# Graph attention scores: one head over all 1024 keys at a time

## The chip, the cores and the metric

The kernel runs on one core of a Trainium2 chip. The metric is the device time of one execution in microseconds; the figure for a kernel is the median over several executions. Engines are written as in the profile: PE is TensorE's matmuls and PEld its weight loads, DVE is VectorE, ACT is ScalarE, POOL is GpSimd, and SP is SyncE, which issues the transfers.

## What is computed

A batch of 16 graph elements, each with 1024 nodes of 64 features and a 1024 x 1024 adjacency matrix, goes through four layers, each with a layer norm and a ReLU ahead and a residual sum behind. Layer 0 thins the adjacency, takes weighted quantiles over the remaining neighbours of each node and applies a small network. Layer 1 takes a mean over neighbours. Layer 2 is attention with eight heads of 64 and the adjacency as a bias. Layer 3 multiplies by the adjacency once more. The change touches layer 2:

```python
qkv = jnp.einsum('bnc,kc->bnk', x, W_qkv)            # 3 x 8 heads x 64
attn = jnp.einsum('bhnd,bhmd->bhnm', q, k) * SCALE   # queries n, keys m
gamma = jnp.exp(x @ W_gamma.T + b_gamma)
attn = g0 * attn + g1 * adj[:, None]                 # g0, g1: per query
attn = jax.nn.softmax(attn, axis=-1)                 # over the 1024 keys
out = jnp.einsum('bhnm,bhmd->bnhd', attn, v).reshape(b, n, H * DIM)
return out @ W_proj.T + b_proj
```

## The kernel before

**Two streams of work.** The generator `picks()` produces layer 0. For each element it makes 96 comparison steps (8 groups of features, 2 halves of nodes, 6 quantile ranks). A step (`compare`, `bits`, `value`) puts three 2048-wide operations on DVE (`le`, `wa`, `wb`, lines 819 to 823), then matmuls `prep` and `val` (line 842) and copies on ACT. Beside the steps `make` builds the tables with the long runs of `px` matmuls (line 735), and `background` does the sorting (lines 577 to 579 forward, 609 to 612 backward) and the thinning for elements to come. For the last two elements nothing is left to sort or thin. The generator `layers()` runs layers 1, 2 and 3 of earlier elements. The loop at the end of the kernel takes turns: each step of `picks` adds 0.42 to what is due, and each part of a layer that is run takes its yielded cost from it (1.0 for one row block of layer 2). When `picks` is exhausted, `alone` is set, and the layers of the last element run by themselves with more buffers. Within this program order a scheduler fixes the order on each engine ahead of the run. Each engine works through its own list in order and waits on semaphores for the others. `adjoining` keeps a group of matmuls next to each other.

**Layer 2.** `h2T` holds the features of an element in columns: rows 0 to 63 are the normalized features h, rows 64 to 127 are h times the per-query factor g0. The loop over `pr` takes the heads in four pairs. For each pair the projections come first (line 1155): keys `kT` from rows 0 to 63 and queries `qT` from rows 64 to 127, both 128 x 1024, with head 0 of the pair in partitions 0 to 63 and head 1 in 64 to 127. Each of two halves of 512 nodes takes one key bank `pk` and one query bank `pq` of PSUM, and each is copied by ACT (line 1162). Then come the values `v`. The loop over `i` takes eight row blocks of 128 queries. In each, the adjacency rows `ad` are loaded and scaled by g1 on ACT. For each half `t` of the keys, two matmuls (line 1190) write the scores of both heads into the two banks of `sp`, one head on each row half of the array (64 rows each). For each head a DVE operation (line 1199) then forms minus the score minus the bias in `s` and takes the minimum over the half. The second half gets the minimum of the first as its starting value, through a pointer operand. The profile calls this operation CUSTOM_DVE_ANT_0 and the write of its minimum `nm` DVE_READ_ACCUMULATOR2_ANT. After both halves, ACT takes the exponential of each head's 1024 scores with the minimum as bias (line 406, `s<-s,nm`). `chunk_cols` transposes them on PE in groups of four (line 459, `pcols`), and ACT copies them to `eT` (line 462). PE multiplies with the values (line 1211, `ao`) and, after a copy, projects (line 1220, `pp`). `residual` adds the result to `xr` after every four row blocks.

**Buffers.** `sp` has one buffer of two PSUM banks; while `alone` is set the second half of the keys goes to two banks `pc` instead. The tags `pb` (two PSUM banks) and, when alone, `pa` serve the projections, transposes and products. `kT` and `qT` have one buffer each. When alone, odd pairs take theirs from the tag `q4`, which has two.

An fp32 matmul appears in the profile as two instructions, its two passes, so each score matmul counts twice in line 1190. A transpose counts once.

Of the kernel before, what the change touches and what calls it, by code (L numbers as in the profile page):

```python
# [8 lines left out]
F32 = mybir.dt.float32  # L9
# [12 lines left out]
P = 128  # L22
# [16 lines left out]
def tile_preln_adj_stack(  # L39
# [30 lines left out]
    nc = tc.nc  # L70
    B, N, D = x.shape
    C = N // P
    H = 8
    HD = W1.shape[1]
    NH = N // 512
# [5 lines left out]
    ps = ctx.enter_context(tc.tile_pool(name="ps", bufs=1, space=PSUM))  # L81
# [9 lines left out]
    def q4(name, shape=(P, N), dt=F32):  # L91
        return sb.tile(list(shape), dt, tag="q4", bufs=2, name=name)
# [7 lines left out]
    def pa(name, shape=(P, 512), dt=F32):  # L100
        return ps.tile(list(shape), dt, tag="pa", bufs=2, name=name)

    def pc_(name, shape=(P, 512), dt=F32):
        return ps.tile(list(shape), dt, tag="pc", bufs=2, name=name)


    alone = []

    def b4(name, shape=(P, N), dt=F32):
        return a4(name, shape, dt) if alone else sb.tile(list(shape), dt, tag="b4", bufs=2, name=name)  # L110

    def pb(name, shape=(P, 512), dt=F32):
        if alone and name != "pcols":
            return pa(name, shape, dt)
        return ps.tile(list(shape), dt, tag="pb", bufs=2, name=name)
# [68 lines left out]
    for c2 in range(2):  # L184
        cols = slice(c2 * BKW, (c2 + 1) * BKW)
# [177 lines left out]
    wqkv = const.tile([P, 2 * H * D], F32, name="wqkv")  # L363
# [5 lines left out]
    for e in range(2):  # L369
        rows = slice(e * D, (e + 1) * D)  # L370
# [19 lines left out]
    sb = ctx.enter_context(tc.tile_pool(name="sb", bufs=1))  # L390
# [11 lines left out]
    def bc(ap, shape):  # L402
        return ap.to_broadcast(list(shape))
# [4 lines left out]
    def adjoining(made):  # L408

        first = next(made)  # L410
        with tc.issue_after(first.ins), tc.high_priority():
            for _ in made:
                pass
# [27 lines left out]
    def to_cols(h, hT, rows):  # L441

        n = h.shape[2]
        for s in range(NH):
            pt = pb("pt", (n, 4, P))
            for c in range(4):
                nc.tensor.transpose(pt[:, c, :], h[:, 4 * s + c, :], identf)
            nc.scalar.copy(hT[rows, s * 512 : (s + 1) * 512], pt[rows].rearrange("d c p -> d (c p)"))
# [663 lines left out]
    def layer2(b, xr):  # L1112
        h = b4("h2", (P, C, 2, D))
        norm_relu(xr, h[:, :, 0, :], b2_)
        hT = sb.tile([P, N], F32, tag="hT2", bufs=1, name="h2T")
        to_cols(h[:, :, 0, :], hT, slice(0, D))
        pg = pb("pg", (P, C, 2))
        for j in range(C):
            nc.tensor.matmul(pg[:, j, :], hT[:D, j * P : (j + 1) * P], wg, start=True, stop=True)
        gm = small("gm", [P, C, 2])  # L1120
        nc.vector.tensor_tensor(gm, pg, bc(bgr[:, None, :], [P, C, 2]), OP.add)
        act(gm, gm, AF.Exp)
        g0 = small("g0", [P, C])
        nc.vector.tensor_scalar(g0, gm[:, :, 0], SCALE, None, op0=OP.mult)

        nc.vector.tensor_tensor(h[:, :, 1, :], h[:, :, 0, :], bc(g0[:, :, None], [P, C, D]), OP.mult)
        to_cols(h.rearrange("p c s d -> p c (s d)"), hT, slice(D, P))
        nc.vector.tensor_tensor(xr, xr, bc(bpr[:, None, :], [P, C, D]), OP.add)
        yield 0.7
        HW = H * D  # L1130
        late = []
        for pr in range(H // 2):

            def residual(i, att, sums):
                rows = xr[:, i : i + C // 2, :]
                rs = small("rs", [P, C // 2, 2], bufs=1)
                nc.vector.reciprocal(rs, sums)
                nc.vector.tensor_tensor(
                    att, att, bc(rs[:, :, :, None], [P, C // 2, 2, D]), OP.mult
                )  # L1140
                for e in range(2):
                    nc.vector.tensor_tensor(rows, rows, att[:, :, e, :], OP.add)

            if alone and pr % 2:
                kT, qT = q4("kT"), q4("qT")
                v = sb.tile([P, C, P], F32, tag="hT", bufs=1, name="v2")
            else:
                kT = sb.tile([P, N], F32, tag="kT", bufs=1, name="kT")
                qT = sb.tile([P, N], F32, tag="qT", bufs=1, name="qT")
                v = sb.tile([P, C, P], F32, tag="v2", bufs=1, name="v2")  # L1150
            for t in range(NH):
                hs = slice(t * 512, (t + 1) * 512)
                both = ((kT, slice(0, D), pb("pk")), (qT, slice(D, P), pb("pq")))
                adjoining(
                    nc.tensor.matmul(
                        pk, wqkv[rows, pr * P : (pr + 1) * P], hT[rows, hs],
                        start=True, stop=True,
                    )
                    for _, rows, pk in both
                )  # L1160
                for dst, _, pk in both:
                    nc.scalar.copy(dst[:, hs], pk)
            for t in range(NH):
                pv = pb("pv2", (P, 4, P))
                for c in range(4):
                    j = 4 * t + c
                    nc.tensor.matmul(
                        pv[:, c, :], hT[:D, j * P : (j + 1) * P],
                        wqkv[:D, HW + pr * P : HW + (pr + 1) * P], start=True, stop=True,
                    )  # L1170
                nc.scalar.copy(v[:, 4 * t : 4 * t + 4, :], pv)
            yield 0.5
            for i in range(C):
                if i % (C // 2) == 0:
                    att = sb.tile([P, C // 2, 2, D], F32, tag="att", bufs=1, name="att")
                    sums = small("sums", [P, C // 2, 2], bufs=2)
                ad = adj_rows(b, i)
                act(ad, ad, AF.Copy, scale=gm[:, i, 1:2])
                eTs = []
                ss = [b4("s") for _ in range(2)]  # L1180
                nms = [None, None]
                for t in range(NH):
                    hs = slice(t * 512, (t + 1) * 512)
                    if alone and t % 2:
                        sps = [pc_("sp") for _ in range(2)]
                    else:
                        sp = ps.tile([P, 2, 512], F32, tag="sp", bufs=1, name="sp")
                        sps = [sp[:, e, :] for e in range(2)]
                    adjoining(
                        nc.tensor.matmul(  # L1190
                            sps[e], qT[e * D : (e + 1) * D, i * P : (i + 1) * P],
                            kT[e * D : (e + 1) * D, hs], start=True, stop=True,
                        )
                        for e in range(2)
                    )
                    for e in range(2):

                        nm = small("nm", [P, 1], bufs=6)
                        nc.vector.tensor_tensor_reduce(  # L1199
                            ss[e][:, hs], sps[e], ad[:, hs], -1.0, 3.0e38 if t == 0 else nms[e],  # L1200
                            op0=OP.add, op1=OP.min, accum_out=nm,
                        )
                        nms[e] = nm
                while late:
                    residual(*late.pop())
                for e in range(2):
                    act(ss[e], ss[e], AF.Exp, bias=nms[e], scale=-1.0, accum_out=sums[:, i % (C // 2), e : e + 1])
                    eTs.append(chunk_cols(ss[e], "eT"))
                ao = pb("ao", (P, P))
                adjoining(  # L1210
                    nc.tensor.matmul(  # L1211
                        ao[e * D : (e + 1) * D, :], v[:, j, e * D : (e + 1) * D], eTs[e][:, j, :],
                        start=j == 0, stop=j == C - 1, tile_position=(0, e * D), skip_group_check=True,
                    )
                    for j in range(C) for e in range(2)
                )
                aT = small("aoT", [P, P], bufs=2)
                nc.scalar.copy(aT, ao)
                pp = pb("pp", (P, 2, D))
                nc.tensor.matmul(pp, aT, wproj[:, pr], start=True, stop=True)  # L1220
                nc.scalar.copy(att[:, i % (C // 2)], pp)
                if (i + 1) % (C // 2) == 0:
                    late.append((i + 1 - C // 2, att, sums))
                yield 1.0
        residual(*late.pop())
# [81 lines left out]
```

## Time and profile before

| | |
|---|---|
| median of 3 runs | 12671.69 us (12668.74 to 12674.88) |
| profiled execution | 12693.13 us, span 12691.3 us |
| PE busy | 11305.5 us, 89% |
| DVE busy | 11575.8 us, 91% |
| ACT busy | 9481.6 us, 75% |
| score matmuls, line 1190 | 4096 passes, 1180.2 us busy |
| minimum operations, line 1199 | 2048 of 128 x 512, 1408.4 us busy in two groups |
| exponentials of scores, line 406 | 1024 of 128 x 1024, 1168.5 us busy |
| query and key copies, line 1162 | 256 of 128 x 512, 151.0 us busy |

In a row of costliest groups the engine, operation, tiles and shapes are followed by the count, then by busy time and mean duration of one, then by the idle time of the engine just before such instructions and what ended most of it. A row of waits gives who waited for whom, the total in us, the number of times and the longest. A row of a table of windows gives the stretch in us from the span's start, its length, the busy time of PE, PEld, DVE, ACT and POOL with the instruction counts, the granted PE clock, the share of DMA time and GB/s. A row of the timeline gives the start, the duration, the engine, line and tiles, and in brackets the idle time before.

### The profile page before, as it was taken

Reading aid. Unit: us, or ns where it says so; the run is one execution under the profiler, and the core shown is the slowest. Engines: PE = TensorE matmul, PEld = TensorE weight load, DVE = VectorE, ACT = ScalarE, POOL = GpSimd, SP = SyncE. Lnnn points to the kernel's source line nnn. Section 1 sums busy time; section 2 is a strip of 40 time slices with the busy share of each in tenths; the row PEclk is TensorE's granted clock in tenths of the full one; section 3 lists DMA queues with packets and bytes.
Section 4 is the critical chain, followed back from the end, with each engine's and each line's share of the span. In section 5 each row is a group of like instructions: output and inputs, shape, how many; then the busy total and the mean of one; then the engine's idle time right before and its main releaser. Section 6 shows DMA issues by size and latency. Waiting matters only on the chain.

```text
span 12691.3 us, 217061 instructions
## 1 busy us (share of the span) xinstructions
PE 11305.5 (89%) x84673; PEld 5334.0 (42%) x84673; DVE 11575.8 (91%) x19682; ACT 9481.6 (75%) x17026; POOL 1.4 (0%) x10
## 2 busy tenths in 40 slices
PE   0778999999899998999989999999999999999988
PEld 0224444444444444444444444444444444444445
DVE  8999989999899999989999999999999899887863
ACT  0557877778777787778877787777777777787866
POOL 0000000000000000000000000000000000000000
PEclk9999999999999999999999999999999999999999
DMA  3012121221212112121221212122121221202121
GB/s 105 28 41 70 54 88 54 74 72 57 83 54 89 59 57 83 53 91 58 68 72 57 89 58 76 63 63 83 55 87 54 62 83 58 94 30 64 34 72 60
DMA packets 503177, 841.09 MB, mean 66 GB/s; under 512 B 238720, under 2 KB 273664, under 8 KB 502144
## 3 DMA queue, kind: packets, MB, share of 16 engines
q1 hardware_dynamic: 502144, 827.20, 20.2%
q8 instruction: 663, 10.86, 0.4%
q14 instruction: 370, 3.03, 0.1%
HBM read 616.27 MB, written 206.57 MB: 65 GB/s over the span
## 4 chain that ended last, share of the span: by engine, by line
DVE 34%; PE 25%; ACT 9%; issue 4%; DMA 1%; ACTq 0%; SPq 0%; DVEq 0%
DVE wa L821 5%; DVE wb L823 5%; DVE le L819 5%; DVE s L1199 5%; PE px L735 4%; DVE vs L869 3%; PE ao L1211 2%; PE pcols L459 2%; DVE bit L857 2%; ACT s L406 2%; PE sp L1190 2%; PE prep L842 2%; PE two L1077 1%; PE agg L875 1%; PE val L842 1%
## 5 line engine op out<-in xcount | busy, mean ns | idle before, releaser
L821 DVE TENSOR_TENSOR wa<-le,c 128x2048 f16<-128x2048 f16 x1536 | 1869.1, 1217 | 211.0 <-PE prep L842 155.3
L735 PE MATMUL px<-valid,cw 128*128 128x512 fp8e4 x8192 | 1978.3, 382 | 0.0
L819 DVE TENSOR_TENSOR le<-cum,krow 128x2048 f16<-128x2048 int16 x1536 | 1864.3, 1214 | 18.2 <-PE val L842 16.1
L823 DVE TENSOR_TENSOR wb<-le,c 128x2048 f16<-128x2048 f16 x1536 | 1867.5, 1216 | 3.0 <-PE prep L842 3.0
L406 ACT ACTIVATE c<-px,shifts 128x512 f16<-128x512 f32 x2048 | 1409.0, 696 | 260.1 <-PE px L756 132.1
L406 ACT ACTIVATE s<-s,nm 128x1024 f32<-128x1024 f32 x1024 | 1168.5, 1143 | 215.7 <-DVE nm L1199 209.4
L735 PEld LDWEIGHTS <-cw 128*128 128x128 f16 x8192 | 802.8, 98 | 1112.4 <-issue 229.7
L1190 PE MATMUL sp<-kT,qT 64*128 64x512 f32 x4096 | 1180.2, 649 | 89.3 <-DVE nm L1199 85.9
L849 ACT COPY wi<-prep 128x512 f32<-128x512 f32 x1536 | 910.3, 593 | 438.8 <-PE prep L842 354.6
L459 PE MATMUL pcols<-identf,s 128*128 128x128 f32 x8192 | 1149.5, 282 | 99.5 <-ACT s L406 50.2
L406 ACT ACTIVATE high<-px,shifts 128x512 f16<-128x512 f32 x1024 | 710.4, 694 | 681.5 <-PE px L735 680.3
L459 PEld LDWEIGHTS pcols<-identf,s 128*128 128x128 f32 x8192 | 894.4, 142 | 652.2 <-ACT eT L462 263.7
L869 DVE SCALAR_TENSOR_TENSOR vs<-pz,vs 128x512 f32<-128x512 f32 x1536 | 1047.8, 682 | 105.5 <-PE pz L862 100.8
L462 ACT COPY eT<-pcols 128x512 f32<-128x512 f32 x2048 | 1112.8, 599 | 30.1 <-PE pcols L459 28.6
L842 PE MATMUL val<-le,tab 128*32 128x512 f16 x12288 | 1089.4, 387 | 19.9 <-DVE vs L869 10.6
L1211 PE MATMUL ao<-eT,v 128*64 128x128 f32 x16384 | 1051.1, 276 | 49.5 <-ACT eT L462 44.3
L406 ACT ACTIVATE vs<-val 128x512 f32<-128x512 f32 x1536 | 935.7, 609 | 152.1 <-PE val L842 72.0
L1211 PEld LDWEIGHTS ao<-eT,v 128*64 128x64 f32 x16384 | 899.5, 137 | 304.0 <-ACT eT L462 247.8
L857 DVE TENSOR_SCALAR bit<-wi,to 128x512 int32<-128x512 int32 x1536 | 827.2, 539 | 0.3 <-ACT cw L406 0.3
L1199 DVE CUSTOM_DVE_ANT_0 s<-sp,ad,nm 128x512 f32<-128x512 f32 x1024 | 726.8, 744 | 108.7 <-PE sp L1190 108.3
L842 PE MATMUL prep<-wb,sel_w 128*32 128x512 f16 x6144 | 649.1, 395 | 178.8 <-DVE wb L823 174.3
L1199 DVE CUSTOM_DVE_ANT_0 s<-sp,ad 128x512 f32<-128x512 f32 x1024 | 681.6, 682 | 130.8 <-PE sp L1190 88.0
(271 smaller groups left out, 18197.4 us busy)
## 6 DMA issues: line engine op xcount, KB each, us to landing
ad<-in_adj_dram SPq DMA_DIRECT2D x768, 512.0 KB
adjT_d<-aT SPq DMA_DIRECT2D x128, 512.0 KB
aT<-adjT_d SPq DMA_DIRECT2D x128, 512.0 KB
md<-sm SPq DMA_DIRECT2D x216, 256.0 KB
sb<-md SPq DMA_DIRECT2D x216, 256.0 KB
rem_d<-rem SPq DMA_DIRECT2D x128, 256.0 KB
left_d<-nb SPq DMA_DIRECT2D x128, 256.0 KB
lr<-left_d SPq DMA_DIRECT2D x256, 128.0 KB
```

What stands on the lines that cost most here:

```text
L406: nc.scalar.activation(out_, in_, func, **kw)
L459: nc.tensor.transpose(pt[:, c, :], ad[:, (4 * s + c) * P : (4 * s + c + 1) * P], identf)
L462: nc.scalar.copy(aT[:, 4 * s : 4 * s + 4, :], pt)
L735: yield nc.tensor.matmul(px[pp], w[:, j, :], valid[:, j, :], start=False, stop=j == C - 1, skip_group_check=True,)
L819: nc.vector.tensor_tensor(le, cum, bc(el.krow[q][:, None, hs], [P, 4, 512]), OP.is_lt)
L821: nc.vector.tensor_tensor(wa, le, c0, OP.mult)
L823: last = nc.vector.tensor_tensor(wb, le, c1, OP.mult)
L842: yield nc.tensor.matmul(dst[32 * pp : 32 * pp + 32, :], w[pp], r[pp], start=i == 2, stop=i in (1, 3), tile_position=(0, 32 * pp), skip_gr ...
L869: nc.vector.scalar_tensor_tensor(vs, pz, 80.0, vs, op0=OP.is_equal, op1=OP.mult)
L1190: nc.tensor.matmul(sps[e], qT[e * D : (e + 1) * D, i * P : (i + 1) * P], kT[e * D : (e + 1) * D, hs], start=True, stop=True,)
L1199: nc.vector.tensor_tensor_reduce(ss[e][:, hs], sps[e], ad[:, hs], -1.0, 3.0e38 if t == 0 else nms[e], op0=OP.add, op1=OP.min, accum_out=nm,)
L1211: nc.tensor.matmul(ao[e * D : (e + 1) * D, :], v[:, j, e * D : (e + 1) * D], eTs[e][:, j, :], start=j == 0, stop=j == C - 1, tile_position ...
```

## The change

Scores are made for one head over all 1024 keys at once. The two row halves of the array now take the two halves of the keys of the same head. `kT` becomes 128 x 2 x 512: partitions 0 to 63 hold keys 0 to 511, partitions 64 to 127 keys 512 to 1023, and the middle index is the head of the pair. The queries have to lie in both partition halves for both heads, so `qT` becomes 128 x 2 x 512 for one half of the nodes (`s`), with head 0 and head 1 crossed: partition half `t` and index `t ^ e` hold head `e`. A new inner function `queries(s, keys)` makes them in two rounds of quadrant matmuls (64 rows x 64 columns). It is called with the keys ahead of the row blocks, and again without the keys at row block 4 for the second half of the queries. One head's two score matmuls fill both banks of `sp`, and one DVE operation over 1024 elements forms `s` and the minimum. When `alone` is set, the second head of each pair goes to two `pc` banks and keeps two operations of 512.

```diff
@@ -1142,24 +1142,44 @@
                     nc.vector.tensor_tensor(rows, rows, att[:, :, e, :], OP.add)
 
             if alone and pr % 2:
-                kT, qT = q4("kT"), q4("qT")
+                kT = q4("kT", (P, 2, 512))
                 v = sb.tile([P, C, P], F32, tag="hT", bufs=1, name="v2")
             else:
-                kT = sb.tile([P, N], F32, tag="kT", bufs=1, name="kT")
-                qT = sb.tile([P, N], F32, tag="qT", bufs=1, name="qT")
+                kT = sb.tile([P, 2, 512], F32, tag="kT", bufs=1, name="kT")
                 v = sb.tile([P, C, P], F32, tag="v2", bufs=1, name="v2")
-            for t in range(NH):
-                hs = slice(t * 512, (t + 1) * 512)
-                both = ((kT, slice(0, D), pb("pk")), (qT, slice(D, P), pb("pq")))
-                adjoining(
-                    nc.tensor.matmul(
-                        pk, wqkv[rows, pr * P : (pr + 1) * P], hT[rows, hs],
-                        start=True, stop=True,
-                    )
-                    for _, rows, pk in both
+
+            def queries(s, keys):
+
+                q = (
+                    q4("qT", (P, 2, 512)) if alone and pr % 2
+                    else sb.tile([P, 2, 512], F32, tag="qT", bufs=1, name="qT")
                 )
-                for dst, _, pk in both:
-                    nc.scalar.copy(dst[:, hs], pk)
+                hs = slice(s * 512, (s + 1) * 512)
+                for r in range(2):
+                    pk, pq = pb("pk") if keys else None, pb("pq")
+
+                    def made():
+                        for n in range(2):
+                            half = slice(n * D, (n + 1) * D)
+                            if keys:
+                                yield nc.tensor.matmul(
+                                    pk[half, :], wqkv[:D, (2 * pr + r) * D : (2 * pr + r + 1) * D],
+                                    hT[:D, n * 512 : (n + 1) * 512], start=True, stop=True,
+                                    tile_position=(0, n * D), skip_group_check=True,
+                                )
+                            hd = 2 * pr + n ^ r
+                            yield nc.tensor.matmul(
+                                pq[half, :], wqkv[D:, hd * D : (hd + 1) * D], hT[D:, hs],
+                                start=True, stop=True, tile_position=(D, n * D), skip_group_check=True,
+                            )
+
+                    adjoining(made())
+                    if keys:
+                        nc.scalar.copy(kT[:, r, :], pk)
+                    nc.scalar.copy(q[:, r, :], pq)
+                return q
+
+            qT = queries(0, True)
             for t in range(NH):
                 pv = pb("pv2", (P, 4, P))
                 for c in range(4):
@@ -1171,6 +1191,8 @@
                 nc.scalar.copy(v[:, 4 * t : 4 * t + 4, :], pv)
             yield 0.5
             for i in range(C):
+                if i == C // 2:
+                    qT = queries(1, False)
                 if i % (C // 2) == 0:
                     att = sb.tile([P, C // 2, 2, D], F32, tag="att", bufs=1, name="att")
                     sums = small("sums", [P, C // 2, 2], bufs=2)
@@ -1179,25 +1201,29 @@
                 eTs = []
                 ss = [b4("s") for _ in range(2)]
                 nms = [None, None]
-                for t in range(NH):
-                    hs = slice(t * 512, (t + 1) * 512)
-                    if alone and t % 2:
-                        sps = [pc_("sp") for _ in range(2)]
+                cols = slice(i % 4 * P, (i % 4 + 1) * P)
+                for e in range(2):
+                    if alone and e:
+                        sps = [pc_("sp") for _ in range(NH)]
                     else:
-                        sp = ps.tile([P, 2, 512], F32, tag="sp", bufs=1, name="sp")
-                        sps = [sp[:, e, :] for e in range(2)]
+                        sp = ps.tile([P, NH, 512], F32, tag="sp", bufs=1, name="sp")
+                        sps = [sp[:, t, :] for t in range(NH)]
                     adjoining(
                         nc.tensor.matmul(
-                            sps[e], qT[e * D : (e + 1) * D, i * P : (i + 1) * P],
-                            kT[e * D : (e + 1) * D, hs], start=True, stop=True,
+                            sps[t], qT[t * D : (t + 1) * D, t ^ e, cols],
+                            kT[t * D : (t + 1) * D, e, :], start=True, stop=True,
                         )
-                        for e in range(2)
+                        for t in range(NH)
                     )
-                    for e in range(2):
+                    if alone and e:
+                        parts = [(sps[t], slice(t * 512, (t + 1) * 512)) for t in range(NH)]
+                    else:
+                        parts = [(sp.rearrange("p t k -> p (t k)"), slice(0, N))]
+                    for s, hs in parts:
 
                         nm = small("nm", [P, 1], bufs=6)
                         nc.vector.tensor_tensor_reduce(
-                            ss[e][:, hs], sps[e], ad[:, hs], -1.0, 3.0e38 if t == 0 else nms[e],
+                            ss[e][:, hs], s, ad[:, hs], -1.0, nms[e] if hs.start else 3.0e38,
                             op0=OP.add, op1=OP.min, accum_out=nm,
                         )
                         nms[e] = nm
```

## The prediction

> **What bounds the kernel now.** I start with the engines' totals and the costliest groups on the page.
>
> ```profile
> PE 11305.5 (89%) x84673; PEld 5334.0 (42%) x84673; DVE 11575.8 (91%) x19682; ACT 9481.6 (75%) x17026; POOL 1.4 (0%) x10
> ...
> L1190 PE MATMUL sp<-kT,qT 64*128 64x512 f32 x4096 | 1180.2, 649 | 89.3 <-DVE nm L1199 85.9
> ...
> L1199 DVE CUSTOM_DVE_ANT_0 s<-sp,ad,nm 128x512 f32<-128x512 f32 x1024 | 726.8, 744 | 108.7 <-PE sp L1190 108.3
> ...
> L1199 DVE CUSTOM_DVE_ANT_0 s<-sp,ad 128x512 f32<-128x512 f32 x1024 | 681.6, 682 | 130.8 <-PE sp L1190 88.0
> ```
>
> DVE and PE are both near full, so an average says little about which of them sets the time. The graph elements give an experiment within the trace. I laid windows from the first `le` of one element to the first `le` of the next. Elements 11, 12, 14 and 15 follow, then the stretch in which layer 2 runs alone.
>
> ```profile
> 8579.00:9323.00 744.00, 689.55 (x5293) 326.27 (x5293) 703.46 (x1232) 594.02 (x1069) 0.00 (x0) 0.99 0.22 68
> 9323.00:10089.00 766.00, 693.37 (x5243) 325.29 (x5242) 735.84 (x1200) 587.63 (x1056) 0.00 (x0) 0.98 0.21 71
> 10847.00:11578.00 731.00, 690.61 (x5239) 325.92 (x5236) 621.51 (x983) 581.09 (x1053) 0.00 (x0) 0.98 0.18 57
> 11578.00:12268.00 690.00, 660.47 (x5151) 313.68 (x5149) 586.15 (x894) 548.46 (x1007) 0.00 (x0) 0.99 0.14 45
> 12268.00:12691.00 423.00, 358.97 (x2776) 246.95 (x2768) 139.99 (x383) 261.09 (x518) 0.00 (x0) 0.88 0.25 82
> ```
>
> The columns are span, then busy PE, PEld, DVE, ACT, POOL. The same windows over elements 2 to 13 average: even ones 772 us long with DVE 733.5 and PE 700 busy; odd ones (3 to 13) 748 us with DVE 704 and PE 693. Element 14 has no sorting or thinning beside it: 731 us, DVE 621.5, PE 691. So 29.5 us of DVE between odd and even cost 24 us (0.82 per us), while 82.5 us between element 14 and the odd ones cost only 17 (0.20). Even elements are paced by DVE, elements 14 and 15 by PE, and odd ones stand at the bend.
>
> Next, the waits around the score operations.
>
> ```profile
> PEld sp L1190 <- DVE nm L1199: 252.2, 307, 3.9
> PEld pcols L459 <- ACT s L406: 248.3, 309, 3.1
> ...
> ACT s L406 <- DVE nm L1199: 209.4, 250, 4.1
> DVE s L1199 <- PE sp L1190: 196.2, 121, 13.2
> ```
>
> PE waits 252 us (338 with the waits of the matmuls themselves) for the minimum before it may overwrite `sp`, and 248 us (298) for the exponentials before the transposes.
>
> **What the Trainium skill says.** "Vector Engine (DVE) Microarchitecture Reference", section 5.2, gives 1.04 ns per column and about 75 ns per instruction once queued. The trace agrees, in starts and not in durations:
>
> ```profile
> 6009.62 0.08 DVE L1199 DVE_READ_ACCUMULATOR2_ANT nm<- 128x1 f32 x1
> 6009.62 0.74 DVE L1199 CUSTOM_DVE_ANT_0 s<-sp,ad,nm 128x512 f32<-128x512 f32 x1
> ...
> 6010.29 0.42 DVE L611 TENSOR_TENSOR sr<-sr,sd 128x512 f16<-128x512 f16 x1
> ...
> 6015.29 0.68 DVE L1199 CUSTOM_DVE_ANT_0 s<-sp,ad 128x512 f32<-128x512 f32 x1
> 6015.90 0.08 DVE L1199 DVE_READ_ACCUMULATOR2_ANT nm<- 128x1 f32 x1
> 6015.90 0.68 DVE L504 TENSOR_TENSOR nb<-nb,rem 128x1024 bf16<-128x1024 bf16 x1
> ```
>
> A 512-wide minimum occupies DVE for 0.61 us (0.533 + 0.077), or 0.67 with the earlier minimum as its pointer operand; the 0.08 accumulator read lies under the next start. "VectorE: DVE Perf Modes", section "Why PSUM operands drop a tier", keeps fp32 from PSUM at one element a cycle, so a merged operation has the same slope. "TensorEngine Tiling (Array Packing)", section "Key Properties", says that tiles load and multiply in parallel and that a change of tiling mode drains the array. The trace supports the first for two tiles: the four passes of a score pair take
>
> ```profile
> 6010.43 1.13 PE L1190 MATMUL sp<-kT,qT 64*128 64x512 f32 x4
> ```
>
> against 4 x 0.59 one by one. Four quadrants at once no row of before shows.
>
> **The change part by part.**
>
> *Minimum operations.* Per pair of heads and row block four of 512 (2 x 0.61 + 2 x 0.67 = 2.56 us) become two of 1024: 1024/0.96 = 1.067, plus 0.077, is 1.144, so 2.29. DVE loses 0.27 us a row block, 32 x 0.27 = 8.7 us an element. I do not take the 292 ns per head that durations and accumulator reads would give. Worth: six even elements x 8.7 x 0.82 = 43; seven odd ones, whose slope lies between 0.20 and 0.82, I take 0.4: 24; elements 14, 15 and the stretch alone (where one head keeps two halves) nothing, since DVE idles there. Together **-67 us**; bounds 12 + 43 = -55 and -107 with 0.82 in both kinds.
>
> *Score matmuls.* Same count, shape and row halves. Two round trips over `sp` per row block before and after. Nothing.
>
> *Projections.* First block: two rounds of one key and one query bank as now, but in quadrants; four concurrent tiles cost what two did, nothing. If column halves ran in turn each round would double, +1 us. The trace's `ao` runs column halves together, so I take nothing. Second block, new, at row block 4: two rounds of query matmuls and two copies per pair. A round is 1.13 us less a tail that overlaps, plus a gap: 1.05. So 2.1 us a pair, **8.4 us of PE an element**, and 8 copies x 0.593 = 4.7 us of ACT. PE's share of the pace is what DVE's leaves: 6 x 8.4 x 0.18 = 9; 7 x 8.4 x 0.6 = 35; elements 14, 15 and alone at full price 25. Together **+70 us**; bounds +35, if half falls into PE's present idle time, and +143 when nothing does. ACT has a fifth of its time free and I cost the copies at zero under the other engines; without that cover they add 16 x 4.7 = 75 us at most.
>
> *The new wait.* Scores of row block 4 need both query copies. Behind them on PE stand the transposes of that row block and layer 0's `prep` and `px` rounds, for which ACT's and DVE's next operations wait. The query tile has one buffer, so its copy waits also for row block 3's scores, already past. I take zero, since the matmuls need only `hT` and can be queued early; bounds: nothing, and two rounds of matmul and copy, 2 x (1.1 + 0.6) = 3.4 us a pair, 218 us.
>
> *Order of the two heads.* Now both minima come after the second key half, then two exponentials (1.14 us each) in a row. After the change head 0's minimum is known one round trip earlier: its exponential runs beside head 1's scores and its transposes beside head 1's minimum. Half of the 298 us of transposes waiting for ACT (149), and about a third of the 338 us before `sp` (110; one DVE operation instead of two with others between), can go. A wait removed in an in-order queue mostly shows up at the next instruction, the `eT` copies before `ao` (292 us now). I count 28%: **-72 us**; bounds 0 and, at 60%, -156.
>
> *Loads, stores, SP's and POOL's queues:* untouched. Tile sizes are the same.
>
> Sum: -67 + 70 - 72 = -69. The profiled execution took 12693.13 us (span 12691.3), 21 above the median 12671.69. I carry the difference over: 12624 for such an execution, about **12600 us** for the median.
>
> **Rivals.** (A) *DVE's saving counts in full*: slope 0.82 in all twelve middle elements and half of the PE block in idle time, waits as above: -107 + 35 - 72 = -144, 12530. For it: DVE is at 95% in even elements. Against: element 14. (B) *A wash*: the heads' new order brings nothing because the next wait takes it all, -67 + 70: 12675. For it: PE-paced elements 14 and 15 give a DVE saving nothing. (C) *Slower through the query block in the middle of a pair*: PE stands in order at row block 4 until ACT, with its own backlog, has copied both banks. Above 69/64 = 1.1 us of stall per pair the gain is gone; with 2.2 us, 141 us are lost and the sum is +72: 12740. For it: PE pays every such stall in full in PE-paced elements. Against: the projections of now wait only 41 us in all for `kT` copies before `pv`. (D) *Quadrants do not run together*: four rounds a pair one us longer, up to 256 us of PE, half of it paid, 12730. Little speaks for it.
>
> **Numbers.** Chances: forecast 0.44, A 0.17, B 0.16, C 0.17, D 0.06. A change under 0.2% (25 us) is about what a measurement of this kernel can't tell from none. The forecast's own range is 12540 to 12650; nearly all of it counts as faster, as does A; B is mostly the same; C and D are slower. Faster 0.60, same 0.16, slower 0.24. The range for 8 in 10 runs from below A (12490) to C (12735).
>
> **What would show it.** Right: 1024-wide minima of about 1.22 us, DVE busy down by some 130 us in starts, PE busy up by about 135, transposes waiting for `s` well under 248 us, even elements shortened more than odd ones, 14 and 15 not shortened. Wrong: score matmuls waiting for `qT` copies in dozens of us (C), `pk` rounds of two us (D), elements 14 and 15 clearly shorter (the wait part undersized), or even elements unchanged (DVE not their pace).

## The result, and the profile after

The changed kernel takes as long as the one before, or slightly longer: median 12693.88 us against 12676.08 us for runs of before beside it, ratio **1.0012**, 95% interval 1.0005 to 1.0018 (the two medians alone would give 1.0014). The forecast was 12600 us, 69 less than before. Its rival B, a wash, gave 12675. The profiled execution after happens to be a short one, 12686.9 us of span, so I read its parts and not its total.

First the totals and the costliest groups of the changed kernel that answer to those shown of before:

```profile
PE 11388.7 (90%) x85694; PEld 5330.6 (42%) x85697; DVE 11450.1 (90%) x17702; ACT 9603.3 (76%) x17158; POOL 1.4 (0%) x10
...
L1225 DVE CUSTOM_DVE_ANT_0 s<-sp,ad 128x1024 f32<-128x1024 f32 (+1 forms) x1024 | 1227.5, 1199 | 275.0 <-PE sp L1212 260.6
...
L1212 PE MATMUL sp<-kT,qT 64*128 64x512 f32 x4096 | 1225.3, 642 | 71.0 <-DVE nm L1225 67.3
```

DVE has 126 us less to do, as forecast, and PE has 83 us and ACT 122 us more. A 1024-wide minimum, from the timeline, lasts 1.22 us, and its accumulator read starts 1.14 us after it:

```profile
6007.68 1.22 DVE L1225 CUSTOM_DVE_ANT_0 s<-sp,ad 128x1024 f32<-128x1024 f32 x1
6008.82 0.08 DVE L1225 DVE_READ_ACCUMULATOR2_ANT nm<- 128x1 f32 x1
```

The windows from one element's first `le` to the next, again for elements 11, 12, 14 and 15 and the stretch in which layer 2 runs alone:

```profile
8558.00:9308.00 750.00, 701.53 (x5357) 327.08 (x5356) 695.48 (x1102) 602.21 (x1076) 0.00 (x0) 0.99 0.21 68
9308.00:10066.00 758.00, 695.50 (x5307) 328.46 (x5306) 725.96 (x1073) 593.79 (x1063) 0.00 (x0) 0.98 0.21 71
10815.00:11539.00 724.00, 689.59 (x5313) 325.21 (x5311) 615.35 (x865) 591.14 (x1060) 0.00 (x0) 0.99 0.17 58
11539.00:12236.00 697.00, 665.86 (x5187) 312.01 (x5187) 575.44 (x763) 553.41 (x1008) 0.00 (x0) 1.00 0.13 45
12236.00:12686.00 450.00, 369.99 (x2856) 247.83 (x2848) 138.15 (x313) 270.15 (x529) 0.00 (x0) 0.88 0.23 78
```

Over all elements the even ones (2 to 12) fell from 772 to 767.5 us and the odd ones (3 to 13) from 748 to about 747. Element 14 fell by 7, element 15 rose by 7, and the last stretch rose from 423 to 450. Three waits from the list of waits of the changed kernel tell where DVE's time went:

```profile
PEld pcols L459 <- ACT s L406: 445.4, 503, 2.9
...
DVE wa L821 <- PE prep L842: 261.5, 170, 4.7
DVE s L1225 <- PE sp L1212: 260.6, 152, 9.2
```

The second of them was, before:

```profile
DVE wa L821 <- PE prep L842: 155.3, 125, 7.0
```

DVE waits 106 us more for `prep` and 64 more for the scores (196 before): both are waits for PE. Transposes wait far longer for the exponentials (248 before), where I had forecast far less.

### The profile page after: what moved, and what is told of

Its sections match the earlier page's. It is cut to its first block, busy times and chain, and to the rows that moved or that the text cites. A ratio compares the mean times of both kernels' runs of the same rounds, so it can differ in the third digit from the quotient of the medians.

```text
span 12686.9 us, 217045 instructions
## 1 busy us (share of the span) xinstructions
PE 11388.7 (90%) x85694; PEld 5330.6 (42%) x85697; DVE 11450.1 (90%) x17702; ACT 9603.3 (76%) x17158; POOL 1.4 (0%) x10
## 5 line engine op out<-in xcount | busy, mean ns | idle before, releaser
L1225 DVE CUSTOM_DVE_ANT_0 s<-sp,ad 128x1024 f32<-128x1024 f32 (+1 forms) x1024 | 1227.5, 1199 | 275.0 <-PE sp L1212 260.6
L1212 PE MATMUL sp<-kT,qT 64*128 64x512 f32 x4096 | 1225.3, 642 | 71.0 <-DVE nm L1225 67.3
L406 ACT ACTIVATE low<-px,shifts 128x512 f16<-128x512 f32 x1024 | 709.5, 697 | 43.4 <-PE px L747 42.3
```

The lines of the kernel that those rows point to most:

```text
L406: nc.scalar.activation(out_, in_, func, **kw)
L1212: nc.tensor.matmul(sps[t], qT[t * D : (t + 1) * D, t ^ e, cols], kT[t * D : (t + 1) * D, e, :], start=True, stop=True,)
L1225: nc.vector.tensor_tensor_reduce(ss[e][:, hs], s, ad[:, hs], -1.0, nms[e] if hs.start else 3.0e38, op0=OP.add, op1=OP.min, accum_out=nm,)
```

## The experiments

Every ratio is to runs of the kernel before on the same chip; 0.001 is 12.7 us. Where two ratios are subtracted, the difference in us is worked out with that. The intervals reach 8 to 17 us to either side, and a difference of two ratios is less sure than either of them. The changed kernel is at 1.0012. Counts over a whole trace are from one execution each.

**The stretch alone (e1).** In the profiled executions the gain of the first stretch and the loss of the last about cancelled. The edit gives pairs that start when layer 2 runs alone the code of before.

```diff
+            old = bool(alone)
+            if old:
...
-                if i == C // 2:
+                if i == C // 2 and not old:
```

> The changed kernel, but pairs of heads that begin when layer 2 runs alone (the last element) use the code of before. Theory 1 (the loss lies in the stretch alone): in the two traces the stretch with layer 0 beside it became 31 us shorter and the stretch alone 27 to 34 us longer (74 instead of 65.7 us a pair), so this kernel should be 25 to 35 us faster than before, ratio 0.9972 to 0.998, with pairs of 65.7 us at the end. Theory 2 (the gain of the first stretch is a chance of one profiled execution, both parts cancel everywhere): equal to before or up to 15 us slower, ratio 1.000 to 1.001.

Measured: 12680.89 us against 12680.17, ratio 1.0003 (0.9995 to 1.0011). The last stretch is back at 419 us in the trace, but by the ratios the kernel is only about 11 us faster than the changed one, and the two intervals overlap. Theory 1's 25 to 35 us below before are not reached; of the two single traces it read too much. How much of the loss lies in the stretch alone is thus not settled by the times, and the first stretch gains nothing that can be told from zero.

**The merge undone (e2), the second query block left out (e3), both (e5).** These three and the changed kernel make a table of two by two.

```diff
-                    if alone and e:
+                    if True:
                         parts = [(sps[t], slice(t * 512, (t + 1) * 512)) for t in range(NH)]
```
```diff
-                if i == C // 2:
-                    qT = queries(1, False)
```

> The changed kernel with two minimum operations of 512 per head, the second with the minimum of the first as pointer operand, in place of one of 1024. DVE gets its 0.27 us a row block back. The prediction's price for it is 67 us: about 12760, ratio to before 1.006. If the DVE saving counts in full (0.82 of 130 us): 1.0095. If the DVE saving is worth nothing because PE paces: 1.001, as the changed kernel.

> The changed kernel without the second query block; row blocks 4 to 7 use the queries of the first half, so this part of the computation is left out. The prediction's price for the block is 70 us: about 12624, ratio to before 0.996. If PE paces everywhere (134 us of PE at full price): 0.991. If the block lies in idle time: 1.001. The pair of heads in the stretch alone shows whether the block explains its 8.4 us: 2 us shorter by the prediction's price, 8 if it is the whole cause.

> The changed kernel with two minimum operations of 512 per head and without the second query block (row blocks 4 to 7 use the queries of the first half, so that part is left out). What remains against before is the layout and the order of the two heads. If the three parts add: after 12694, less 132 for the block (the run without it), plus 73 for the split (the run with it) is 12635, ratio to before 0.9965. The prediction's price for the order of heads (72 us): 0.9943. If the order of heads brings nothing, 1.000, and block and merge do not add.

| ratio to before (95% interval) | with second block | without |
|---|---|---|
| merged minimum | 1.0012 (1.0005 to 1.0018) | 0.9910 (0.9897 to 0.9924) |
| two minima per head | 1.0070 (1.0057 to 1.0082) | 0.9987 (0.9981 to 0.9994) |

Read along the rows, the block costs 0.0102 (129 us) with the merge and 0.0083 (105 us) without. Read down the columns, the merge gains 0.0058 (74 us) with the block and 0.0077 (98 us) without. What remains with neither, the new layout and the order of the heads, gains 0.0013, **16 us**, where the prediction had 72. In sum -16 - 98 + 129 = +15: the measured 0.0012. The merge is worth what was forecast or more. The block costs nearly twice its forecast 70 us, and that alone turns a gain of 0.9% into nothing. That the two costs of the block and the two gains of the merge differ by 24 us is not clear of the intervals. In the stretch alone the traces have 65.7 to 67.2 us for a pair of heads before, 72.5 to 74.2 after and 68.1 to 71.0 in e3, so the block is rather more than half of what a pair lost there.

**What the block's 129 us consist of (e6, e9).** First the matmuls of the block without their copies, then matmuls and copies, the copies into a spare tile that nobody reads (the `else` branch stands in e9 alone).

```diff
-                    qT = queries(1, False)
+                    queries(1, False)
...
+                    else:
+                        spare = small("spare", [P, 512], HP, bufs=1)
+                        nc.scalar.copy(spare, pq)
```

> The changed kernel with the matmuls of the second query block but without their copies; row blocks 4 to 7 use the queries of the first half, so that part is left out. The block costs 132 us in all. Theory 1 (PE time at full price, 64 pairs x 2.1 us = 134): this kernel stays near the changed one, ratio to before 1.000. Theory 2 (the wait of row block 4 for ACT and the copies' own ACT time make half of it or more): 0.995 or less. 0.991 would say that PE's part is free.

> The changed kernel with matmuls and copies of the second query block, but the copies go to a spare tile that nothing reads (fp16, for want of room), and row blocks 4 to 7 use the queries of the first half, so that part is left out. Matmuls alone stood at 0.9958, the whole block at 1.0012. Theory 1 (the rest is ACT's time, 128 copies x 0.6 = 75 us, at nearly full price): 1.000 or more. Theory 2 (the rest is the wait of row block 4's scores for the copies): 0.996 to 0.997. The trace of the changed kernel shows only 49 us of such waits, so I expect between 0.998 and 1.000.

Measured: 0.9958 (0.9946 to 0.9971) and 0.9968 (0.9956 to 0.9980). From 0.9910 upwards: the matmuls cost 0.0048, **61 us**; the copies 0.0010, 13 us, which the intervals don't separate from nothing; and using the result the remaining 0.0044, **56 us**. So e6's theory 1 falls (PE time at full price would be 134), and e9's theory 2 holds. My own guess for e9 was too high. That e3 landed on 0.991, the number of "134 us of PE at full price", was chance: the matmuls are less than half of what it measured.

The tile view of `qT` shows the wait: idle time by what ended it, first in the changed kernel, then in e9. The first line of each is ACT's idle time before query copies (e9's view does not hold the copies into the spare tile, before which ACT idles 32 us), the last one is PE's.

```profile
  PE pq L1171: 49.9, 85
  ACT qT L1179: 49.0, 82
```
```profile
  PE pq L1171: 11.3, 12
...
  ACT qT L1179: 4.1, 10
```

PE waits 49 us for the query copies in the changed kernel and 4 us where nothing uses them. A piece of the changed kernel's timeline shows how, at row block 4 of a pair:

```profile
5132.32 1.07 PE L1171 MATMUL pq<-h2T,wqkv 64*64 64x512 f32 x4
...
5133.62 0.60 ACT L1179 COPY qT<-pq 128x512 f32<-128x512 f32 x1
5133.66 0.19 PEld L1171 LDWEIGHTS pq<-h2T,wqkv 64*64 64x64 f32 x4 [0.24 <-issue]
5133.66 1.08 PE L1171 MATMUL pq<-h2T,wqkv 64*64 64x512 f32 x4
...
5134.66 0.29 PEld L1212 LDWEIGHTS sp<-kT,qT 64*128 64x128 f32 x2 [0.81 <-ACT qT L1179]
5134.66 1.88 PE L1212 MATMUL sp<-kT,qT 64*128 64x512 f32 x4
5134.78 0.58 ACT L1179 COPY qT<-pq 128x512 f32<-128x512 f32 x1 [0.56 <-PE pq L1171]
5135.42 0.29 PEld L1212 LDWEIGHTS sp<-kT,qT 64*128 64x128 f32 x2 [0.46 <-ACT qT L1179]
```

The first score matmul needs only the first copy and goes ahead. The second needs the other copy, and its weights are loaded 0.76 us later. So the two share the array only in part, and the group takes 1.88 us instead of 1.13. I call a group torn when its second instruction starts over 0.1 us after the first (otherwise it is 0.007 us). Counted in the traces, of the 64 first score groups of a row block 4 the changed kernel has 58 torn ones, the kernel before 1, e9 2. The mean length of the 64 from first start to last end is 1.84 us, 1.14 before and 1.13 in e9, and in 12 of the 58 other matmuls stand between the two. The busy time of all score matmuls is 1225 us, 1180 before and 1184 in e9. Waiting for the queries thus has a part beside PE's idle time: torn pairs of score matmuls, 64 x 0.7 = 45 us by which these groups are longer, some 7 us of it used by the other matmuls in between.

The block also parts two row blocks that overlapped. Over the 60 pairs that begin beside layer 0, row block 4's first scores stood on average 2.2 us ahead of row block 3's first `ao` matmul before the change. In the changed kernel they come 10.7 us behind it, in e9 1.6. From row block 3's first scores to row block 4's it takes 27.1 us instead of 17.6; the next row block follows after 11.4 instead of 16.8, so only part of the delay is made up. Nor do the matmuls of the block come early: the first starts 13.3 us (median) after row block 3's last scores, when the query tile is free, and in none of the 64 pairs before row block 3's `ao` had ended. The copies follow their matmuls by 0.05 us (median). So neither the single query tile nor other work of ACT made the queries late; PE came to the block late. Whether that is its place in PE's order or the two `pb` banks, which row block 3's products use ahead of it, no run tells. Idle time, torn pairs and delayed row blocks overlap and can't be added up to the 56 us.

**The wait taken away by making all queries early (e11, e12).** In e11 all queries are made at the head of the pair, in two tiles (two buffers of the tag `qT`, in the stretch alone too), and the adjacency rows have two buffers instead of three, to make room. The control e12 has that last change alone.

```diff
-            qT = queries(0, True)
+            qTs = [queries(0, True), queries(1, False)]
...
-                if i == C // 2:
-                    qT = queries(1, False)
+                qT = qTs[i // 4]
```

> The changed kernel with both halves of the queries made at the head of the pair, in two query tiles; to make room the adjacency rows have two buffers in place of three. Nothing is left out and PE's and ACT's work is that of the changed kernel. Against the run with two adjacency buffers alone: if the wait of row block 4 for its queries is the missing 56 us of the block, this kernel is 40 to 60 us faster; if the 56 us are something else (bank traffic, PE order), the two are equal within 15 us.

> The changed kernel with two adjacency buffers in place of three, the control for the run with all queries first. If loads are early enough: 1.001, as the changed kernel; if a scaled row tile comes late, slower.

Measured: 0.9990 (0.9982 to 0.9998) and 1.0033 (1.0021 to 1.0046). With equal work, making the queries early saves 0.0043, 55 us, as much as the 56 us that e9 left. Row block 4's torn first groups fall from 57 to 3, and its scores come 1.8 us behind row block 3's `ao` instead of 11.1. The run changes the place of the block and the number of query tiles at once. The third adjacency buffer is worth 0.0021, 27 us; the first of my two cases for the control was wrong.

**The order of the heads (e4, e10).**

```diff
-                    eTs.append(chunk_cols(ss[e], "eT"))
+                for e in range(2):
+                    eTs.append(chunk_cols(ss[e], "eT"))
```

> The changed kernel with the transposes of both heads written after both exponentials, as far as program order goes. In the changed kernel transposes wait 561 us for the exponentials (298 before), since head 0's transposes are queued right behind head 1's scores. Theory 1 (this wait is what ate the gain of the earlier head): waits for the exponentials fall towards 300 us and the kernel is 30 to 70 us faster than the changed one, ratio to before 0.995 to 0.999. Theory 2 (the row block is not on the path that sets the pace; the wait only stands where another would): within 15 us of the changed kernel, 1.000 to 1.002.

Measured: 1.0013 (1.0006 to 1.0019), the changed kernel's time. But PE's order hardly moved: from the exponential of head 0 to its transposes the mean is 2.04 us, 2.02 in the changed kernel. The edit did not do what it was to do, so this run tells the two theories apart in nothing. The next edit holds both heads' exponentials until both minima are there; head 1's exponential and transposes then come first:

```diff
-                for e in range(2):
-                    act(ss[e], ss[e], AF.Exp, bias=nms[e], scale=-1.0, ...)
+                first = None
+                for e in (1, 0):
+                    with tc.issue_after(first.ins) if first else ExitStack():
+                        first = nc.scalar.activation(ss[e], ss[e], AF.Exp, bias=nms[e], ...)
```

> The changed kernel with head 1's exponential ahead of head 0's on ACT, so that both wait for both minima, as before the change. Nothing is left out. The prediction gave the earlier head 72 us: about 12766, ratio to before 1.007. The runs without merge and block left 16 us for layout and order together: 1.002 to 1.003. If the early head hurts, because its transposes block PE while they wait for the exponential: 1.000 or less.

Measured: 1.0026 (1.0016 to 1.0036), 18 us slower than the changed kernel, in line with the 16 us of the table; the two intervals just touch. From the lists of waits, first of the changed kernel, then of this one:

```profile
PEld pcols L459 <- ACT s L406: 445.4, 503, 2.9
...
PEld pcols L459 <- ACT eT L462: 55.6, 92, 1.5
```
```profile
PEld pcols L459 <- ACT s L1235: 268.3, 342, 2.7
PEld pcols L459 <- ACT eT L462: 266.1, 465, 2.4
```

The weight loads of the transposes wait 177 us less for the exponentials and 210 us more for the copies `eT`: the wait moved and was not saved, and the kernel is slower. The trace tells the same of the row blocks. Over the 60 pairs beside layer 0, the mean from a row block's first scores to its first `ao` fell from 20.0 to 15.3 us with the change, and from there to the next row block's first scores it rose from 3.6 to 8.2 (change of pair included); the sum stayed within 0.1 us of 23.5. That the order in which the two streams are interleaved sets that pause is an inference; no run changed it.

**A version that beats both (e7, e8).** The block is needed only because each head's queries must lie in both partition halves. Here they are made once, with one copy per half of the nodes as before, and two transfers per row block put 128 queries of each head into the other half (`qx`; `qs` is the pair of the natural columns of `q` and `qx`).

```diff
-                if i == C // 2:
-                    qT = queries(1, False)
...
+                x_ = small("qx", [P, P], bufs=2)
+                for n in range(2):
+                    nc.sync.dma_start(
+                        x_[(1 - n) * D : (2 - n) * D, :], q[n * D : (n + 1) * D, i * P : (i + 1) * P]
+                    )
...
-                            sps[t], qT[t * D : (t + 1) * D, t ^ e, cols],
+                            sps[t], qs[t ^ e][t * D : (t + 1) * D, :],
```

> The changed kernel with the queries made once, as before, and one query copy for each half of the nodes; for each row block two transfers of 32 KB put the two heads' 128 queries into the other partition half, two row blocks ahead. No part of the computation is left out. PE and ACT work is that of the run without the second block. If the block's PE and ACT time was the cost: ratio to before 0.991 to 0.993, faster than both kernels. If the transfers come late or hold the adjacency loads up on SP's queue: 0.996 or more, with score matmuls waiting for DMA.

> As the run with queries crossed by DMA, but pairs of heads that begin when layer 2 runs alone use the code of before. In the run without the second block the stretch alone took 431 us, with the code of before 419 to 423: 8 to 12 us faster than the run crossed by DMA, ratio to before about 0.990 to 0.992. If the transfers delay the stretch alone, more than that.

Measured: 0.9921 (0.9908 to 0.9933), and with the code of before in the stretch alone **0.9903** (0.9889 to 0.9916), 12562.94 us: 124 us less than before. The list of DMA issues of e8 has the transfers, and its tile view of `qx` what score matmuls wait for:

```profile
qx<-qT SPq DMA_DIRECT2D x960, 32.0 KB
```
```profile
  DVE nm L1272: 138.2, 204
  issue: 84.7, 217
  DMA qx<-qT: 8.8, 6
```

960 small transfers cost 9 us of waiting and take the place of a block that cost 129. By the ratios, e7 stands 0.0011 or 14 us above e3, which has no second queries at all; the intervals overlap.

## Why the prediction was wrong

The sum had four terms: -67, +70, 0 and -72, together -69. Measured, with the block there or not: -98 to -74, +61, +69 and -16. Two steps failed: the zero for the new wait, and the -72 for the order of the heads.

- **Minimum operations.** The duration and start-to-start time were right, and the price was near: -67 against -74 and -98. Its distribution over the elements was not, so the total owes something to luck. I gave nothing to elements 14 and 15, since DVE has idle time there; with the minima split again (e2) element 14 takes 740 us instead of 724, and element 15 706 instead of 697, in single traces. A likely reason, not tested: sorting and thinning, which element 14 lacks, lie off the path of the row blocks, and the minimum lies on it. What removing one kind of DVE work saves then says little about another kind.
- **Score matmuls.** "Nothing" was wrong at row block 4, where pairs are torn. Their time is part of the wait's 56 us below.
- **First block.** Right: where all its `pk` and `pq` passes start together, in 37 of 128 rounds, the four quadrants start within 0.02 us of each other, and a round of the second block takes 1.08 us, so rival D falls. The Trainium skill's "TensorEngine Tiling (Array Packing)", section "Key Properties", which has tiles run in parallel, is borne out for four. What I overlooked: head 0's scores now need both query copies at once, and the first score group of a pair is torn in 27 of 64 pairs, 17 before (mean 1.66 us against 1.29). This lies within the measured -16.
- **Second block's matmuls.** +70 against 61: right in kind and size.
- **Bounds.** Two of my sums were off. With 0.82 for both kinds the six even and seven odd elements give 13 x 8.7 x 0.82 = -93, not -107, so rival A should have been about 12540. The second block at full price is 16 x 8.4 = 134, not 143. The forecast of 12600 does not use either.
- **The new wait, with the copies that make it,** is the first step that failed. I saw both and took nothing for either: the copies because ACT has time to spare, the wait because the matmuls "can be queued early". They were not early. PE came to them a median 13.3 us after the query tile was free, behind row block 3's `ao`, and row block 4's scores, which had run ahead of that `ao`, had to follow. Measured 13 us for the copies, which is not told from nothing, and 56 for the wait. Rival C had this wait, at 0.9 us a pair (56/64) instead of 2.2, but not its reason: ACT took up the copies almost at once. By itself it stays under the 1.1 us from which I let it decide; together with the next failure it decides.
- **The order of the heads** is the second, -72 against -16. I took waits counted in the profile and cashed 28% of them. A row block's own chain from scores to `ao` did get 4.7 us shorter, but on average the next one was not begun sooner.
- Of the signs that I named, DVE's loss (126 us) and the even elements' lead held. PE's busy time rose by 83 us instead of 135. The transposes' wait went the other way, and element 14 became shorter. Of the signs of being wrong, scores waiting for `qT` copies in dozens of us came true (49 us).

## What to carry to other kernels

Two halves of a trade that look equal in engine time are not: work that is put between two steps that overlapped costs its time, its wait, the pairing of what stands behind it and the overlap. A zero for the wait needs more than a free buffer: it needs a place in the engine's order at which the work does run early, and a trace of the kernel before shows what stands in front of that place. A wait counted in a profile is not money: e10 removed 177 us of one kind, gained 210 us of the next and lost 18. When a layout needs the same data in another partition half, look for a queue that has room, here SP's transfers, before giving the copy to the engines that pace the kernel.

## What was not expected of the hardware

Two matmuls on the two row halves share the array only as far as both are ready together. Where their operands came from copies that ended some 1.1 us apart, the group took 1.88 us instead of 1.13, and the mean over the first groups of all row blocks 4 was 1.84. The two 32 KB transfers per row block between partition halves were nearly always there in time two row blocks ahead, 9 us of waiting for 960 of them.
